# Six kinds of transposes and spreads moved from TensorE to VectorE and transfers through HBM, in a four-block transformer on one core

## The chip, the cores and the metric

The kernel runs on one core of one Trainium2 chip. The metric is the device time in microseconds, from the launch to the end of the program. The core's engines have their own instruction queues and run beside each other: TensorE (PE; its weight loads are listed as PEld), VectorE (DVE), ScalarE (ACT), GpSimd (POOL) and SyncE (SP). In this kernel SP issues all DMA transfers. An engine takes its instructions in the order written; where one waits for another engine or for a DMA, everything behind it on that engine waits too.

## The reference

The input x has 8 batches of 512 tokens of 256 float32 values. Six residual blocks follow each other:

```python
x = x + 0.5 * fp4_ffn(layernorm(x))          # gate/up/down, each operand quantised in blocks of 16
x = x + retention(layernorm(x))              # 4 blocks of 128 tokens with decay
x = x + 0.5 * fp4_ffn(layernorm(x))
x = x + 0.5 * soft_moe(layernorm(x))         # 1024 slots
x = x + attention(layernorm(x))              # 16 heads of 16, causal, low-rank additions to the weights
x = x + 0.5 * soft_moe(layernorm(x))         # the same weights again

def soft_moe(x):                             # gamma and rms norms left out
    logits   = einsum("bsd,etd->bset", xn, se)
    dispatch = softmax(logits, axis=1)                       # over the tokens
    slots    = einsum("bsd,bset->betd", xn, dispatch)
    processed = gelu(slots @ w1) @ w2
    combine  = softmax(logits.reshape(b, s, e * t), axis=-1) # over the slots
    return einsum("bnd,bsn->bsd", processed.reshape(b, e * t, d), combine)
```

## The kernel before

All matrices are float32. A batch's x stays in SBUF as 4 tiles of 128 tokens by 256 values. TensorE contracts over the partitions, so whatever was made with tokens on the partitions has to be turned before it can be contracted over its features. The kernel does this with `nc.tensor.transpose` against an identity, into PSUM, and a copy out of PSUM to SBUF.

**Three lanes.** The work of a batch is cut into units, and three lanes work on different batches at once. Lane "front" runs, for a batch, the first ffn, retention, the second ffn and the dispatch part of the first soft MoE. Lane "back" runs attention and the second dispatch. Lane "experts" runs the two large products over the slots and mixes the result back into x, for both soft MoEs. The last two batches use lanes front and back for their attention side by side. Four batches have room in SBUF; a new one is loaded when an old one has been mixed for the second time and stored.

**The order.** Instructions are written out by a planner. `Meter` keeps a modelled time of each engine; each generator step (`yield banks, needs, token`) says which PSUM rooms it wants ("p" is a pair of banks, of which there are three, "o" a single bank, of which there are two), which tokens must be done, and which token it makes. `drive` emits the next step of the lane that is able to start and has had the least of TensorE's time. Work for VectorE that may wait is kept in chains (`Chain`, `lane.later`) and put between, by `put_off`. The order is thus fixed when the program is built; on the chip each engine follows it. Every operation passes `Meter.emit`, so line 161 is the line of all instructions in the profile, and the groups are told apart by their tiles.

**The places that the change touches**, with the names of their PSUM tiles:

- `columns` (line 445): 8 transposes turn a batch's 4 tiles of 128x256 into yT, 2 x 128 x 512 (`tr_m` in dispatch, `tr_cx_a` for the context in attention; also `tr_r` in retention and `tr_a` at the head of attention), and ACT copies them out.
- `dispatch` (line 840): logits `lt` = seT by yT, with slots on the partitions. VectorE copies them to lg and takes each slot's maximum over the tokens (smax). `maxima` spreads these: `spread` transposes a column repeated 128 times, so that each partition has all slots' maxima in a row (`sm_m`). `turned` turns the logits (`l_m`), takes sm off and makes the exponentials ed. The maxima of each token over the slots (most) are spread in the same way (`nm_m`), and `less` and `combine` make the mixing weights from them. `slots(q)` makes 256 slots at a time (`sl_m`), and `slots_turned(q)` turns them with 4 transposes into slT (`slT_m`).
- `experts` (line 961): `h_e` = w1 by slT, gelu, `p_e` = w2 by that, `mo_e` mixes with lg.
- `attention` (line 1019): four rounds n of 4 heads. `largest` makes scores (`s_a`) and their maxima, negated, in a zeroed tile nmx at columns that stand for rows of q. `lower(n)` turns nmx (4 transposes, `mx_a`) and adds it to qv, so that the maximum is taken off inside the next product. `weights` makes the scores the other way round (`st_a`), then come exponentials and values (`c_a`), and `tokens_again` (`ct_a`). Finally `columns` turns the context cx, and `o_a` projects it.

Of the kernel before, what the change touches and what calls it, by code (L numbers as in the profile page):

```python
# [69 lines left out]
class Meter:  # L70
# [7 lines left out]
    BYTES, LANDS = 270e3, 1.8  # L78
    STRETCH = 3.413
    HOLE = 0.3  # L80

    def __init__(self, nc):
        self._nc = nc
        self.at = dict.fromkeys(("PE", "DVE", "ACT", "POOL", "SP"), 0.0)
        self._written, self._used = {}, {}
        self._table, self._mode = None, None
        self.end, self.last = 0.0, None
        self.moved = 0.0

        self.stretch, self.worked, self.full = self.STRETCH, 0.0, False  # L90

        self.banks = set()

        self.holds = {"DVE": [], "POOL": []}

        self.kept, self.fill = None, None
        self.tensor = _Engine(self, "PE", nc.tensor)
        self.vector = _Engine(self, "DVE", nc.vector)
        self.scalar = _Engine(self, "ACT", nc.scalar)
        self.gpsimd = _Engine(self, "POOL", nc.gpsimd)  # L100
        self.sync = _Engine(self, "SP", nc.sync)
# [10 lines left out]
    @staticmethod  # L112
    def _pieces(x):

        pitch, free = x.ap[0][0], x.ap[1:]
        first = x.offset % pitch if pitch else x.offset
        last = first + sum(s * (n - 1) for s, n in free)
        return [(x.tensor.name, k) for k in range(first // 512, last // 512 + 1)]

    def begins(self, engine, aps):  # L120

        at = self.at[engine]
        for x in aps:
            for k in self._pieces(x):
                who, t = self._written.get(k, (engine, 0.0))
                at = max(at, t if who == engine else t + self.HOP)
        for k in self._pieces(aps[0]):
            who, t = self._used.get(k, (engine, 0.0))
            at = max(at, t if who == engine else t + self.HOP)
        return at  # L130

    def emit(self, engine, op, call, args, kwargs):
# [18 lines left out]
        if engine == "SP":  # L151

            self.moved = max(self.moved, at) + int(np.prod(aps[0].shape)) * 4 / self.BYTES
            at = self.moved + self.LANDS
# [101 lines left out]
class Chain:  # L256
# [3 lines left out]
    def __init__(self, steps, needs=(), places=None):  # L260
        self.steps, self.needs, self.places = list(steps), needs, places
        self.place = None

        self.ready = 0.0

# [4 lines left out]
def macaron(ctx: ExitStack, tc: tile.TileContext, a: dict, out: bass.AP):  # L270
# [7 lines left out]
    slab = ctx.enter_context(tc.tile_pool(name="slab", bufs=1))  # L278
    ctx.enter_context(tc.manual_schedule())
# [88 lines left out]
    nmx = []  # L368
    for u in range(2):
        t = const.tile([P, NT, P], FP, tag=f"nmx{u}", name=f"nmx{u}")  # L370
        nc.gpsimd.memset(t, 0.0)
        nmx.append(t)

# [71 lines left out]
    def columns(lane, src, name):  # L445

        ps = pair(f"tr_{name}")
        for c in range(NT):
            for d in range(KD):
                nc.tensor.transpose(ps[:, d, c * P : (c + 1) * P], src[c][:, d * P : (d + 1) * P], ident)  # L450
        dst = wide(lane, f"yT_{name}", KD, S)
        nc.scalar.copy(dst, ps)
        return dst
# [37 lines left out]

    def quantise_later(lane, v, room, n, name, token, needs=()):
        def tiles(n, name):
            return [
                small.tile([P, n], FP, tag=f"{kind}{n}_{lane.name}_{chain.place}", name=f"{kind}_{name}", bufs=1)
                for kind in ("scale", "rec")
            ]

        steps = quantise_steps(v, room, n, name, tiles)
        chain = Chain([(None, step) for step in steps[:-1]] + [(token, steps[-1])], needs, lane.places)  # L500
        lane.later.append(chain)

    def project(dst, yT, w, o):

        for d in range(KD):
            nc.tensor.matmul(dst, w[:, d, o * P : (o + 1) * P], yT[:, d, :], start=(d == 0), stop=(d == KD - 1))

    def project_tokens(dst, yT, w, tiles=range(NT)):

        for t in tiles:  # L510
            for d in range(KD):
                nc.tensor.matmul(
                    dst[:, t // 2, (t % 2) * D : (t % 2 + 1) * D],
                    yT[:, d, t * P : (t + 1) * P],
                    w[:, d, :],
                    start=(d == 0),
                    stop=(d == KD - 1),
                )
# [244 lines left out]
    def retention(lane, b, after):  # L763
        nm = f"r_{b}"
        y = ys.pop(b)
        yield "p", tuple(y["tokens"]), ("yT", nm)
        yT = columns(lane, y, nm)
# [62 lines left out]
    def spread(ps, cols, n):  # L830

        for c in range(n):
            nc.tensor.transpose(ps[:, c * P : (c + 1) * P], cols[:, c : c + 1].to_broadcast([P, P]), ident)

# [5 lines left out]
    def dispatch(lane, b, tag, ep):  # L840
# [4 lines left out]
        yield "p", tuple(y["tokens"]), ("yT", nm)  # L845
        yT = columns(lane, y, nm)
# [17 lines left out]
        def maxima(h):  # L864
            ps = one(f"sm_{nm}_{h}")
            spread(ps, smax[:, h * NT : (h + 1) * NT], NT)
            sm[h] = narrow(lane, f"sm_{nm}_{h}", S)
            nc.scalar.copy(sm[h], ps)
# [20 lines left out]
        for h in range(2):  # L889
            yield "o", (("lt", nm, 2 * h), ("lt", nm, 2 * h + 1)), ("sm", nm, h)  # L890
# [6 lines left out]
        yield "o", (("ed", nm, 0, 0), ("ed", nm, 0, 1), ("ed", nm, 1, 0), ("ed", nm, 1, 1)), ("nm", nm)  # L897
        ps = one(f"nm_{nm}")
        spread(ps, most[:, 0, :], NT)
        tm = narrow(lane, f"tm_{nm}", S)  # L900
        nc.scalar.copy(tm, ps)

        def less(j):
            hs = lg[:, j : j + 2, :]
            nc.vector.tensor_tensor(hs, hs, tm.unsqueeze(1).to_broadcast([P, 2, S]), ALU.add)

        def combine(j):
# [6 lines left out]
                + [(("cw", nm) if j == NS - 2 else None, lambda j=j: combine(j)) for j in range(0, NS, 2)]  # L914
# [4 lines left out]
        def slots(q):  # L919
# [13 lines left out]
            sls[q] = narrow(lane, f"sl_{nm}_{q}", 2, D)  # L933
            for c in range(2):
                nc.vector.tensor_scalar(sls[q][:, c, :], ps[:, c, :D], rs[:, c, :], None, ALU.mult)

        def slots_turned(q):
            ps = one(f"slT_{nm}_{q}")
            for d in range(KD):
                for c in range(2):  # L940
                    nc.tensor.transpose(
                        ps[:, d * QS + c * P : d * QS + (c + 1) * P], sls[q][:, c, d * P : (d + 1) * P], ident
                    )
            slT = ep.tile([P, KD, QS], FP, tag="slT", name=f"slT_{nm}_{q}", bufs=4)
            nc.scalar.copy(slT, ps.rearrange("p (d n) -> p d n", d=KD))
            slTs.append(slT)
# [4 lines left out]
        for q in range(NQ + 1):  # L951
            if q < NQ:
                yield "p", (("nm", nm),) if q < NQ - 1 else (("cw", nm),), ("sl", nm, q)
                slots(q)
            if q:
                yield "o", (("sl", nm, q - 1),), ("slT", b, tag, q - 1)
                slots_turned(q - 1)
# [3 lines left out]
    def experts(lane, b, tag, ep):  # L961
# [4 lines left out]
        for q in range(NQ):  # L966
            hids = []
            for m in range(NH // 4):
                yield "p", (("slT", b, tag, q),), ("h", nm, q, m)
                ps = pair(f"h_{nm}_{q}_{m}")  # L970
                for c in range(4):
                    for d in range(KD):
# [3 lines left out]
                            slTs[q][:, d, :],  # L976
# [20 lines left out]
        for i in range(NT):  # L997
            yield "o", tuple(("p", nm, q) for q in range(NQ)), None
# [20 lines left out]
    def attention(lane, b, after):  # L1019
# [5 lines left out]
        yield "p", tuple(y["tokens"]), ("yT", nm)  # L1025
        yT = columns(lane, y, nm)
        qv, kv = {}, {}
# [64 lines left out]
        def largest(n, k):  # L1092

            u = n % 2
# [4 lines left out]
            ps = four(f"s_{nm}_{n}_{k}", qv[n], kv[n], parts, causalb)  # L1099
            for g in range(2):  # L1100
                for i, c in by_query[k]:
                    cols = nmx[u][:, i, :].rearrange("p (r f) -> p r f", f=32)
                    nc.vector.tensor_reduce(
                        cols[:, 2 * g : 2 * g + 2, HD * (1 - u)],
# [6 lines left out]
        def lower(n):  # L1111

            ps = one(f"mx_{nm}_{n}")
            for i in range(NT):
                nc.tensor.transpose(ps[:, i * P : (i + 1) * P], nmx[n % 2][:, i, :], ident)
            nc.vector.tensor_tensor(qv[n], qv[n], ps, ALU.add)
# [53 lines left out]
        yield "o", tuple(("s", nm, 0, k) for k in range(NK)), ("q", nm, 0)  # L1170
        lower(0)
        ctxT = None
        for n in range(N):
# [23 lines left out]
            if n + 1 < N:  # L1197
                yield "o", tuple(("s", nm, n + 1, k) for k in range(NK)), ("q", nm, n + 1)
# [3 lines left out]
        yield "p", tuple(("cx", nm, n) for n in range(N)), ("cxT", nm)  # L1202
        cxT = columns(lane, [cx[:, t, :] for t in range(NT)], f"cx_{nm}")
        for g in range(NT // 2):
            yield "o", (("cxT", nm),), None
            ps = one(f"o_{nm}_{g}")
            for t in (2 * g, 2 * g + 1):
                for d in range(KD):
                    nc.tensor.matmul(
                        ps[:, (t % 2) * D : (t % 2 + 1) * D],  # L1210
                        cxT[:, d, t * P : (t + 1) * P],
# [27 lines left out]

    def put_off(by):  # L1240
# [3 lines left out]
        for lane in lanes:  # L1244
            for chain in lane.later:
                free_place = chain.places is None or chain.place is not None or chain.places
                if chain.ready <= by and free_place and all(t in done for t in chain.needs):
                    found.append((lane, chain))
                    break
        return min(found, key=lambda x: x[0].spent, default=None)  # L1250
# [67 lines left out]
    def drive(until=lambda: False):  # L1318
        while not until():
# [6 lines left out]
            now = nc.at["PE"]  # L1326
            if nc.at["DVE"] <= now + 0.5:
# [7 lines left out]
            if ready:  # L1335
# [3 lines left out]
            found = put_off(max(nc.at["DVE"], min(first, min(  # L1339
                (c.ready for lane in lanes for c in lane.later), default=first))))  # L1340
# [99 lines left out]
```

## Time and profile before

| what | value |
|---|---|
| median of 3 runs | 3043.21 us (3041.76 to 3046.69) |
| the profiled execution's own time | 3046.74 us |
| its span, first to last instruction | 3044.9 us |
| granted TensorE clock, mean | 0.987 |
| HBM read and written | 11.87 MB, 4.19 MB |
| instructions | 36364 |

How to read it: the busy time of an engine is the union of its instructions' durations. Matmuls are pipelined, so that the mean duration of one is longer than the time by which it moves the next; a group's busy time is counted by the union. A row of the groups gives line, engine, operation, output<-inputs, shapes, count, then busy us and mean ns, then the idle time of the engine just before these instructions and what ended it. A row of the windows gives the stretch in us, its width, then the busy time of PE, PEld, DVE, ACT and POOL, each with its number of instructions, the granted clock, the DMA share and GB/s. A row of the timeline or of the chain gives start and length in us.

### The profile page before, as it was taken

The numbers are of one execution on the slowest core, as the hardware profiler recorded it, in microseconds if no ns is written. First come the engines' busy times: TensorE is split into PE (matmuls) and PEld (weight loads), VectorE is DVE, ScalarE is ACT, GpSimd is POOL, SyncE is SP. The second block draws the span as 40 slices with busy tenths as digits, with TensorE's granted clock in tenths as the row PEclk, the third lists the DMA queues.
The fourth block names the chain that finished last, engine by engine and source line by source line (L and its number), as shares of the span: only waits on it lengthen the run. The fifth ranks groups of instructions, "written<-read, shape, count | busy, mean of one in ns | idle before, by whom it ended". The sixth has DMA issues, their size and how long they took to land.

```text
span 3044.9 us, 36364 instructions
## 1 busy us (share of the span) xinstructions
PE 2913.4 (96%) x14958; PEld 2141.7 (70%) x14958; DVE 1631.3 (54%) x3767; ACT 1122.7 (37%) x1443; POOL 127.9 (4%) x231
## 2 busy tenths in 40 slices
PE   5789999999999999999999999999999999999999
PEld 3556777667776678767777678766787677675778
DVE  7676656455564563555636556465645654445240
ACT  3223433334334333433424335253443433333321
POOL 0000000000000000000000000000000000000000
PEclk8989999999999999999999999999999999999999
DMA  4000000000000000000000000000000000000000
GB/s 129 0 1 1 1 1 1 1 1 1 1 1 1 15 1 1 1 1 15 1 1 1 1 14 1 1 1 1 15 1 1 1 1 8 1 1 1 8 1 14
DMA packets 16806, 18.39 MB, mean 6 GB/s; under 512 B 2048, under 2 KB 16128, under 8 KB 16640
## 3 DMA queue, kind: packets, MB, share of 16 engines
q1 hardware_dynamic: 16640, 16.07, 1.6%
q8 instruction: 118, 1.93, 0.3%
q14 instruction: 48, 0.39, 0.0%
HBM read 11.87 MB, written 4.19 MB: 5 GB/s over the span
## 4 chain that ended last, share of the span: by engine, by line
PE 90%; DVE 6%; ACT 3%; issue 1%; SPq 0%; DMA 0%; POOL 0%; ACTq 0%; DVEq 0%; POOLq 0%
PE p_e L161 15%; PE h_e L161 14%; PE gu_f L161 10%; PE lt_m L161 7%; PE sl_m L161 7%; PE mo_e L161 7%; PE dn_f L161 5%; PE s_a L161 4%; PE st_a L161 3%; PE c_a L161 2%; PE qk_a L161 2%; PE l_m L161 1%; PE hTp_f L161 1%; PE y_r L161 1%; PE a_r L161 1%; PE k_r L161 1%
## 5 line engine op out<-in xcount | busy, mean ns | idle before, releaser
L161 PE MATMUL h_e<-slT_m,w1g 128*128 128x256 f32 x2048 | 464.9, 381 | 6.1 <-DVE nmx L161 3.1
L161 PE MATMUL p_e<-w,hid_e 128*128 128x256 f32 x2048 | 455.2, 380 | 0.9 <-DVE x L161 0.9
L161 PEld LDWEIGHTS p_e<-w,hid_e 128*128 128x128 f32 x2048 | 385.8, 190 | 64.2 <-issue 10.6
L161 PEld LDWEIGHTS h_e<-slT_m,w1g 128*128 128x128 f32 x2048 | 381.8, 190 | 67.6 <-issue 6.0
L161 PE MATMUL gu_f<-w_in,y_ffn 128*128 128x352 f32 x1024 | 334.8, 480 | 13.0 <-ACT y_ffn L161 9.7
L161 ACT ACT_TABLE_LOAD x210 | 269.4, 1283 | 109.7 <-PE h_e L161 40.0
L161 PEld LDWEIGHTS gu_f<-w_in,y_ffn 128*128 128x128 f32 x1024 | 200.1, 199 | 126.1 <-issue 17.4
L161 DVE TENSOR_REDUCE nmx<-s_a 128x2 f32<-128x256 f32 (+3 forms) x256 | 196.0, 818 | 136.8 <-PE s_a L161 136.4
L161 ACT ACTIVATE pT_a<-st_a 128x1024 f32<-128x1024 f32 (+1 forms) x192 | 158.9, 879 | 239.4 <-DVE st_a L161 222.3
L161 PE MATMUL mo_e<-proc_e,lg_m 128*128 128x257 f32 x1024 | 234.5, 382 | 1.9 <-DVE x L161 1.2
L161 ACT ACTIVATE hid_e<-h_e 128x1024 f32<-128x1024 f32 x128 | 131.0, 1023 | 277.8 <-PE h_e L161 277.6
L161 PE MATMUL sl_m<-y_dis,ed_m 128*128 128x257 f32 x1024 | 232.9, 380 | 0.1
L161 PE MATMUL lt_m<-yT_m,seT 128*128 128x512 f32 x512 | 229.7, 596 | 2.5 <-ACT yT_m L161 2.1
L161 PEld LDWEIGHTS mo_e<-proc_e,lg_m 128*128 128x128 f32 x1024 | 191.2, 190 | 35.4 <-issue 3.3
L161 PEld LDWEIGHTS sl_m<-y_dis,ed_m 128*128 128x128 f32 x1024 | 190.3, 190 | 29.8 <-issue 2.1
L161 PE MATMUL dn_f<-w_dn,hT_f 128*128 128x256 f32 x768 | 179.2, 386 | 1.2 <-DVE x L161 0.8
L161 DVE TENSOR_SCALAR_CACHE_REDUCE lg_m<-lt_m 128x512 f32<-128x512 f32 x128 | 84.5, 688 | 176.4 <-PE lt_m L161 176.3
L161 DVE TENSOR_TENSOR h_f<-h_f,gu_f 128x352 f32<-128x352 f32 x128 | 66.4, 520 | 209.9 <-ACT h_f L161 209.0
L161 PEld LDWEIGHTS lt_m<-yT_m,seT 128*128 128x128 f32 x512 | 94.8, 190 | 112.1 <-issue 100.1
L161 ACT COPY proc_e<-p_e 128x512 f32<-128x512 f32 x64 | 37.5, 586 | 351.8 <-PE p_e L161 351.8
L161 PEld LDWEIGHTS dn_f<-w_dn,hT_f 128*128 128x128 f32 x768 | 144.5, 194 | 24.0 <-DVE st_a L161 1.7
L161 DVE TENSOR_TENSOR st_a<-st_a,causalT 128x256 f32<-128x256 f32 x256 | 100.9, 428 | 96.8 <-PE st_a L161 90.3
(199 smaller groups left out, 3457.5 us busy)
## 6 DMA issues: line engine op xcount, KB each, us to landing
x<-in_L_attn_x SPq DMA_DIRECT2D x8, 512.0 KB, 5.7
out<-x SPq DMA_DIRECT2D x8, 512.0 KB, 2.9
w1g<-in_L_ffn_w SPq DMA_DIRECT2D x1, 1024.0 KB, 6.3
se<-in_L_ffn_slot_embeds SPq DMA_DIRECT2D x1, 1024.0 KB, 9.7
w<-in_L_ffn_w SPq DMA_DIRECT2D x1, 1024.0 KB, 12.2
dn<-in_L_ffn_w_down SPq DMA_DIRECT2D x1, 704.0 KB, 9.0
gu<-in_L_ffn_w_gate SPq DMA_DIRECT2D x1, 640.0 KB, 5.1
gu<-in_L_ffn_w_up SPq DMA_DIRECT2D x1, 640.0 KB, 6.4
```

The lines of the kernel that those rows point to most:

```text
L161: call(*args, **kwargs)
```

## The change

Six of the twelve kinds of transposes and spreads leave TensorE. The turning of yT in dispatch, of the context in attention and of the slots is done in blocks of 32 by 32 by VectorE (`nc.vector.transpose`), which turns each block in its place. The blocks then lie in the wrong partitions; four DMAs write them to HBM so that each row there is a row of the turned matrix, and one DMA brings it back to the same tile. The columns in the tile then have another order than before, and the products read it with steps (`tile`, `all`). The spreads of smax and most, and the maxima of attention, go out to HBM element by element as a row, and come back repeated over the partitions, or into the rows of q. In attention this replaces the addition, since the rows of q that take the maxima are written directly.

```diff
+    def through_hbm(turn, dst, n, name):
+        def away():
+            turn()
+            t["d"] = d = dram.tile([P, NB, n], FP, tag=f"d{n}", name=f"d_{name}", bufs=6)
+            z = dst().rearrange("p (b n) -> p b n", b=NB)
+            to = d.rearrange("(b i) a n -> i b a n", b=NB)
+            for k in range(NB):
+                nc.sync.dma_start(out=to[:, :, k, :], in_=z[BLK * k : BLK * (k + 1)])
+        def back():
+            nc.sync.dma_start(out=dst(), in_=t["d"].rearrange("p a n -> p (a n)"))
...
+    def spread_later(lane, cols, dst, k, needs, token, name):
+        def away():
+            t["d"] = d = dram.tile([1, P * n], FP, tag=f"row{n}", name=f"row_{name}", bufs=6)
+            nc.sync.dma_start(out=k(d), in_=cols)
+        def back():
+            nc.sync.dma_start(out=dst(), in_=t["d"].to_broadcast([P, t["d"].shape[1]]))
...
 class Columns:   # later(): what dispatch (order "d t j") and cx ("j d t") now use
+                v = self.t.rearrange(f"p (b {order}) -> p t d b j", b=NB, d=KD, t=NT)
+                for c in range(NT):
+                    blocks(v[:, c], self.src[c].rearrange("p (d b i) -> p d b i", d=KD, b=NB))
...
         def lower(n):
-            ps = one(f"mx_{nm}_{n}")
-            for i in range(NT):
-                nc.tensor.transpose(ps[:, i * P : (i + 1) * P], nmx[n % 2][:, i, :], ident)
-            nc.vector.tensor_tensor(qv[n], qv[n], ps, ALU.add)
+            def away():
+                t["d"] = d = dram.tile([NG, S], FP, tag="row_mx", name=f"row_{nm}_{n}", bufs=6)
+                nc.sync.dma_start(
+                    out=d.rearrange("r (i p) -> p (r i)", p=P), in_=nmx[n].rearrange("p r i -> p (r i)")
+                )
+            def back():
+                nc.sync.dma_start(out=qv[n][HD * (1 - n % 2) :: 32, :], in_=t["d"])
...
         def slots_turned(q):
+            def turn():
+                slT = ep.tile([P, KD * QS], FP, tag="slT", name=f"slT_{nm}_{q}", bufs=4)
+                blocks(
+                    slT.rearrange("p (n j) -> p n j", j=BLK), sls.pop(q).rearrange("p (n i) -> p n i", i=BLK)
+                )
...
-                            slTs[q][:, d, :],
+                            slTs[q].rearrange("p (a d c j) -> p d c a j", a=NB, d=KD, c=2)[:, d],
...
-                yield "p", (("nm", nm),) if q < NQ - 1 else (("cw", nm),), ("sl", nm, q)
+            yield "p", tuple(("ed", nm, q // 2, g) for g in range(2)), ("sl", nm, q)
...
-            yield "o", tuple(("p", nm, q) for q in range(NQ)), None
+            yield "o", tuple(("p", nm, q) for q in range(NQ)) + (("cw", f"m{tag}_{b}"),), None
```

The way out and the way back are two steps of a chain. Steps that only send are not treated as VectorE's work: `drive` issues them (`to_send`) as soon as, in the planner's time, their needs are there. Chains with a block transpose come before VectorE's other put-off chains (`first`). The planner's time of a transfer becomes the larger of its bytes at 270 GB/s and 3 ns for each contiguous run (`RUN`), and 1.8 us to land (`LANDS`), after the transfers before it. A row in HBM is one piece for the planner (`far`), so that the way back waits for the whole way out. The products of attention's head and of retention keep their transposes on TensorE, and so do the logits, the ffn's rows and hidden values and the context's return to tokens.

## The prediction

> **What bounds the kernel now.** I read the page first (busy shares, slices, the chain that ended last), then the groups by line, the chain of its last part, the window sums, and the DMA view and SP's timeline for what a transfer costs.
>
> ```profile
> PE 2913.4 (96%) x14958; PEld 2141.7 (70%) x14958; DVE 1631.3 (54%) x3767; ACT 1122.7 (37%) x1443; POOL 127.9 (4%) x231
> PE   5789999999999999999999999999999999999999
> PEclk8989999999999999999999999999999999999999
> PE 90%; DVE 6%; ACT 3%; issue 1%; SPq 0%; DMA 0%; POOL 0%; ACTq 0%; DVEq 0%; POOLq 0%
> ```
>
> TensorE is busy from the third slice to the last, at nearly full clock, and makes 90% of the chain. No other engine passes 54%. In the middle little is idle:
>
> ```profile
> 120.00:500.00 380.00, 350.25 (x1465) 258.63 (x1464) 241.49 (x578) 126.31 (x182) 21.07 (x37) 0.96 0.00 1
> 500.00:2500.00 2000.00, 1964.52 (x10338) 1439.67 (x10337) 1105.78 (x2558) 786.33 (x983) 83.94 (x148) 1.00 0.01 3
> 2900.00:3045.00 145.00, 139.51 (x645) 116.15 (x643) 31.80 (x71) 30.80 (x35) 1.50 (x3) 1.00 0.02 8
> ```
>
> First number after the width: PE busy. It idles 35 us in the 2000 us of the middle, 30 us between 120 and 500, 5 us at the end. A microsecond taken off TensorE is a microsecond of the end, as long as its next work is there.
>
> **What leaves TensorE.** The six kinds, by the groups (busy us and mean ns, then the idle before them):
>
> ```profile
> L161 PE MATMUL slT_m<-ident,sl_m 128*128 128x128 f32 x256 | 38.3, 275 | 3.0 <-DVE qv_a L161 0.9 <-ACT slT_m L161 0.7 <-DVE cx_a L161 0.6
> L161 PE MATMUL sm_m<-ident,smax_m 128*128 128x128 f32 x128 | 19.4, 278 | 5.3 <-DVE qv_a L161 2.3 <-ACT sm_m L161 2.0 <-DVE lg_m L161 0.5
> L161 PE MATMUL mx_a<-ident,nmx 128*128 128x128 f32 x128 | 19.4, 274 | 0.0
> L161 PE MATMUL tr_m<-ident,y_dis 128*128 128x128 f32 x128 | 16.6, 273 | 0.1
> L161 PE MATMUL nm_m<-ident,most_m 128*128 128x128 f32 x64 | 9.7, 275 | 1.0 <-DVE x L161 1.0
> L161 PE MATMUL tr_cx_a<-ident,cx_a 128*128 128x128 f32 x64 | 8.5, 274 | 0.5 <-DVE cx_a L161 0.5
> ```
>
> That is 768 transposes. What one is worth is the first choice. The mean is 274 ns, and the Trainium skill ("TensorE: Matmul & The Clock Gate", Part 4: PE-mode transpose) gives about 275 ns in a kernel: trace and page agree on the duration, which would make 768 x 0.275 = 211 us. But the durations overlap; the chain shows the time by which one moves the next:
>
> ```profile
> 2907.04 0.87 PE tr_m L161 x8
> ...
> 2911.37 13.73 PE lt_m L161 x32
> 2925.11 0.44 PE sm_m L161 x4
> ...
> 2954.86 0.44 PE slT_m L161 x4
> ```
>
> 0.87 / 8 = 0.44 / 4 = 0.109 us. So 768 x 0.109 = **83.7 us**, and that I take. The idle before these groups, 3.0 + 5.3 + 0.1 + 1.0 + 0.5 = **9.9 us**, goes with them.
>
> **What leaves and joins the others.** ACT loses the copies out of PSUM (rows: slT_m 37.0, sm_m 18.4, yT_m 16.2, tm_m 9.4, yT_cx_a 8.1: 89 us); at 37% this is worth nothing. POOL loses two memsets of 0.5 us at the start. DVE loses the 32 additions of mx_a (21.8 us) and gains block transposes: 16 x 4 and 8 x 4 of 128x256, and 64 of 128x512. No row shows one. The nearest are an SBUF-to-SBUF tensor_scalar of 128x256 (y_dis, 409 ns) and an addition of 128x512 (qv_a, 682 ns): 96 x 0.41 + 64 x 0.68 = 83 us, net +61 us, so 1692 us of about 2985, 57%. Half or double these durations makes net +20 or +144 us (60%). I take +61 and charge nothing: it runs while TensorE works for other lanes. Without that cover, each dispatch would pay 4 x 0.41 + 0.68 = 2.3 us and each attention 1.6, 50 us in all. The matmuls' count and sizes stay; only their operands' steps change (rival 3).
>
> **What SP and the DMA gain.** Each turned matrix takes four DMAs out and one back, each spread one and one: (16 + 8 + 64) x 5 + (32 + 16 + 32) x 2 = 600 issues where the program now has 48. At the 0.38 us of an x store's issue that is 228 us, on an SP that sleeps. More weighs the way back, which waits on SP until the way out has landed, with all later transfers behind it, x's loads and stores too. Durations: a 512 KB store of x lands 3.0 us after issue and a load 4.2 (the DMA view of 1000 to 1100 us); 256 KB (wT_q) 2.8; a few KB (gx) 2.1. Elements of 4 bytes are the uncertain part. The nearest row is gamma's load, which moves 4 bytes a packet (DMA view, 16.5 to 17.4 us):
>
> ```profile
> DMA packets 281, 0.00 MB, mean 1 GB/s; under 512 B 281, under 2 KB 281, under 8 KB 281
> q1 hardware_dynamic: 281, 0.00, 15.6%
> ```
>
> 0.9 us / 281 = one packet per 3.2 ns, each 0.156 x 16 x 0.9 / 281 = 8 ns of an engine: they come slower than the engines could take them. So 2048 maxima of attention take 6.6 us, 512 of dispatch 1.6. Round trips, as estimates from these rows: yT and cxT 3.5 + 4.2 = 7.7; slT, half the bytes, 6.0; a spread of dispatch 1.6 + 2.1 + 2.8 = 6.5; attention's maxima 6.6 + 2.1 + 2.1 = 10.8 us. Over 24, 64, 48 and 32 trips: 1227 us, 41% of the span even if none overlapped. SP is no bound, but a trip will sometimes queue.
>
> Those rows are loads; none shows a 4-byte store to HBM. Here a rule speaks against the change: the Trainium skill ("DMA: Bandwidth & Descriptors", Specifications) says a transfer under 512 B is a read-modify-write, and its section "Latency and other measured facts" puts an HBM access at 0.2 us. If each of the 128 writes per engine waited for that, the maxima would take 25.6 us instead of 6.6, 19 us late x 32 = 608 us. I take the row, since the engines keep many packets in flight there; below it nothing can be gained, because what paces them stays.
>
> **What covers the trips.** Maxima to weights in attention is the tightest, from the last scores (s_a) to the first weights (st_a):
>
> ```profile
> 2609.76 0.40 PE L161 MATMUL s_a<-causalb,identb 128*128 128x128 bf16 x4
> ...
> 2610.83 3.75 PE L161 MATMUL sl_m<-y_dis,ed_m 128*128 128x257 f32 x16
> 2614.41 0.60 PE L161 MATMUL mx_a<-ident,nmx 128*128 128x128 f32 x4
> ...
> 2615.28 3.64 PE L161 MATMUL sl_m<-y_dis,ed_m 128*128 128x257 f32 x16
> 2618.86 1.14 PE L161 MATMUL st_a<-qv_a,kv_a 32*128 32x512 f32 x8
> ```
>
> Already 8.8 us lie between them, filled by another lane; over all 32 such gaps the median is 8.6 us, from 3.3 to 16.9. The trip needs 10.8 us, so the order has to put one or two more groups of other lanes there. It is written out anew with the trip in it (3 ns a run, 1.8 us to land: my rows say 3.2 ns and 2.1 us), so it should. Slots no longer wait for the spread of the row maxima, only the last mixing does. yT, cxT and slT have experts' groups of 3.5 to 6.9 us beside them.
>
> I charge: 168 trips x 0.1 us = 17 us (the present hand-overs of slT_m and sm_m idle 8.3 us over 96 groups, 0.09 each); 6 us in the first dispatch, where only two lanes run; 12 us at the end, where the last dispatch has one lane of experts beside it and three of its trips (7.7 + 6.5 + 6.0 = 20 us) may outlast it. Uncovered, a trip costs its whole length.
>
> Sum: -83.7 - 9.9 + 17 + 6 + 12 = -58.6. The profiled execution took 3046.7 us (span 3044.9), so 2988; it lies 3.5 above the median of the three runs, so **2984 us**.
>
> **Rivals.** (1) *Slower: attention's maxima come late.* PE takes instructions in order; if st_a waits for q, all three lanes wait behind it. It decides when the 32 trips are late by 58.6 / 32 = 1.8 us each beyond the order's figure, i.e. if a 4-byte write takes 4.1 instead of 3.2 ns. At 5.2 ns each trip is 4 us late: 2984 + 32 x 4 = 3112 us. For it: the write has no row, and the rule above. Against: the load row has the engines at a sixth of their time.
>
> (2) *The lanes become bound by latency.* Batch 4 is loaded at 1033.2 and stored at 2517.1 us: 1484 us of life, four batches in flight, a new one only when an old one is stored. The trips add to a life about 4 x 9.7 in attention, 7.5 for cxT, 2 x 19 in the dispatches: 84 us. Were it all exposed, the period grows by 21 us, 168 us over eight batches; a quarter of it gives 2984 + 42 = 3026. For it: every lane already works through. Against: TensorE, not the lanes' waits, fills the time now, and the scheduler gives a lane that is behind the first place.
>
> (3) *The new steps in the operands cost TensorE.* h_e and lt_m now read runs of 32 floats; cxT's weights every eighth float. At 10% more, h_e (2048 x 0.216) and lt_m (512 x 0.429) lose 66 us: 3050, no gain. No row of before has such steps; runs of 128 bytes make it unlikely. At double, the 128 loads of o_a (190 ns) exceed their matmuls by 0.16: 21 us. Below nothing there is no reason.
>
> **Chances.** The forecast 0.62 (2950 to 3020), rival 1 0.18, rival 2 0.15, rival 3 0.05. A measurement of this kernel tells about 0.2%, 6 us, from no change. Faster by more: the forecast, most of rival 2: 0.75. Within: 0.04, from rivals 2 and 3. Slower: rival 1 and the bad end of 2: 0.21. Range 2945 to 3085: below, all trips are hidden and some other idle goes; above, rival 1 beyond 3 us a trip.
>
> **What would show it.** Right: PE some 84 us less busy, six groups gone, h_e and lt_m at 381 and 596 ns; about 8 us from issue to landing of the maxima's store; idle before st_a, l_m and h_e under 20 us in sum; DVE near 1690. Wrong: waits of st_a or l_m for a DMA over 50 us (rival 1), slices of PE below 9 throughout (2), longer means of h_e or lt_m (3).

## The result and the profile after

The changed kernel takes 3424.06 us (median of 4 runs, 3416.32 to 3427.10) against 3043.15 us before: 1.1246 times as long, 95% interval 1.1223 to 1.1268. I had forecast 2984 us, and 2945 to 3085 as the range. The direction was wrong, and the rival that ends on the slow side named a part of the mechanism, but less than a fifth of the loss (69 of 381 us).

The page of the kernel after, the same lines as before:

```profile
PE 2956.4 (86%) x14190; PEld 2138.8 (62%) x14190; DVE 1691.2 (49%) x3895; ACT 1099.8 (32%) x1354; POOL 127.8 (4%) x229
PE   5787999788999899878988979989799887876878
PEclk8898999899999899998999989999899999997989
PE 62%; DMA 23%; DVE 9%; ACT 3%; issue 2%; SPq 1%; POOL 0%; DVEq 0%; ACTq 0%; POOLq 0%
```

TensorE executes 768 instructions fewer and is nevertheless busy 43 us longer. The chain of which PE made 90% now has 23% of DMA in it. The sum closes on the spans, 3424.9 - 3044.9 = 380 us: TensorE's idle time rises from 131.5 to 468.5 us, +337, and its busy time by 43, which is the 83.7 us that the transposes freed and 127 us by which the rest became slower. The windows show that no stretch is spared (first after the width: PE busy; third from the end: granted clock):

```profile
500.00:3000.00 2500.00, 2211.22 (x10940) 1593.76 (x10939) 1245.94 (x2872) 834.31 (x1001) 94.09 (x162) 0.94 0.13 24
3000.00:3425.00 425.00, 334.55 (x1653) 247.12 (x1651) 124.39 (x282) 102.47 (x108) 5.97 (x12) 0.89 0.14 28
```

What TensorE waits for (total us, times, longest us; the five largest), then what SP's queue waits for, as far as it waits for a transfer to land:

```profile
PE st_a L170 <- DMA qv_a<-row_a: 124.9, 25, 7.0
PE lt_m L170 <- DMA yT_m<-d_yT_m: 54.4, 7, 13.3
PE l_m L170 <- DVE most_m L170: 46.0, 9, 9.4
PE tr_f L170 <- DVE y_ffn L170: 45.8, 15, 7.4
PE gu_f L170 <- ACT y_ffn L170: 38.6, 13, 11.0
```

```profile
SPq L170 <- DMA row_a<-nmx_a: 342.3, 32, 11.4
SPq L170 <- DMA row_sm_m<-smax_m: 293.4, 32, 11.5
SPq L170 <- DMA row_nm_m<-most_m: 99.2, 15, 10.3
SPq L170 <- DMA d_slT_m<-slT_m: 44.5, 57, 3.8
```

The second list is the key to the first. A way back cannot be issued before its way out has landed: that takes 342.3 / 32 = 10.7 us of waiting for attention's 2048 maxima, but also 293.4 / 32 = 9.2 us for the spreads of dispatch, which have only 512 elements. From issue to issue the medians in SP's timeline are 11.4 us (row_a), 9.8 (row_sm_m) and 9.8 (row_nm_m). The order counts on 8.3, 3.7 and 3.7, and my estimates were 8.7, 3.7 and 3.7. yT's blocks, with 64 times the bytes of the maxima, are hardly late: 3.9 us from the first of yT's four stores to the issue of its load (median), where my estimate for the way out was 3.5. cxT's take 10.1 all the same, because SP stands in between until a spread has landed; with the spreads back on TensorE (below) they take 3.8.

The waits for most_m and y_ffn (before: 1.4 us at l_m, 24.4 at tr_f, 9.7 at gu_f) have grown by the spreads at second hand. VectorE also takes its work in order, and it stands before ed_m and lg_m:

```profile
DVE ed_m L170 <- DMA sm_m<-row_sm_m: 135.9, 24, 12.9
DVE lg_m L170 <- DMA tm_m<-row_nm_m: 56.8, 14, 7.2
```

Behind it the other lanes' work (l_m's PSUM, the ffn's rows) waits too. The run below that has only the spreads back on TensorE shows it: there l_m waits 2.9 us for most_m, tr_f 21.8 and gu_f 5.9 for y_ffn. One stretch of the chain shows how a late trip is paid twice:

```profile
1411.88 11.26 DMA row_a<-nmx_a
...
1423.21 1.99 DMA qv_a<-row_a
...
1425.33 2.09 PE st_a L170 x8
1427.43 9.29 PE p_e L170 x32
```

The scores had ended at 1410.6. TensorE did 8 us of other work, stood idle for 6.7 us, and then the 32 matmuls of p_e took 9.29 us, where the same 32 take 6.91 us in the trace of before. p_e's operands did not change; TensorE ran slower after the gap. The clock records of the trace give 1.0 up to 1421.6 us, 0.5 from there to 1431.8, and then 1.0 again; in these two traces they have no other value. Over the program the granted clock fell from 0.987 to 0.928. TensorE was busy at 0.5 for 68.4 us before and for 320.6 us after; at half the clock, work takes twice as long, so that half of the 252 us more is lost: 126 us, which are the 127 us by which its work became slower.

### The profile page after: what moved, and what is told of

Same layout as the page of the kernel before. It is cut to its first block, busy times and chain, and to the rows that moved or that the text cites. A ratio compares the mean times of both kernels' runs of the same rounds, so it can differ in the third digit from the quotient of the medians.

```text
span 3424.9 us, 36030 instructions
## 1 busy us (share of the span) xinstructions
PE 2956.4 (86%) x14190; PEld 2138.8 (62%) x14190; DVE 1691.2 (49%) x3895; ACT 1099.8 (32%) x1354; POOL 127.8 (4%) x229
## 4 chain that ended last, share of the span: by engine, by line
PE 62%; DMA 23%; DVE 9%; ACT 3%; issue 2%; SPq 1%; POOL 0%; DVEq 0%; ACTq 0%; POOLq 0%
PE h_e L170 10%; PE p_e L170 10%; PE gu_f L170 7%; DMA row_a<-nmx_a 7%; DMA row_sm_m<-smax_m 6%; PE lt_m L170 5%; PE sl_m L170 5%; PE dn_f L170 4%; PE mo_e L170 4%; PE s_a L170 3%; PE st_a L170 3%; DMA yT_m<-d_yT_m 2%; DMA row_nm_m<-most_m 2%; DMA sm_m<-row_sm_m 2%; PE c_a L170 2%
## 5 line engine op out<-in xcount | busy, mean ns | idle before, releaser
L170 PE MATMUL h_e<-slT_m,w1g 128*128 128x256 f32 x2048 | 481.9, 392 | 33.5 <-DMA slT_m<-d_slT_m 14.1
L170 PE MATMUL p_e<-w,hid_e 128*128 128x256 f32 x2048 | 471.2, 390 | 0.9 <-DVE cx_a L170 0.3
L170 PEld LDWEIGHTS h_e<-slT_m,w1g 128*128 128x128 f32 x2048 | 397.1, 197 | 108.7 <-issue 41.1
L170 PEld LDWEIGHTS p_e<-w,hid_e 128*128 128x128 f32 x2048 | 398.8, 196 | 70.6 <-issue 13.1
L170 ACT ACT_TABLE_LOAD x257 | 329.7, 1283 | 150.9 <-PE h_e L170 68.4
L170 DVE TENSOR_REDUCE nmx_a<-s_a 128x2 f32<-128x256 f32 (+3 forms) x256 | 196.0, 818 | 205.0 <-PE s_a L170 204.4
L170 PE MATMUL lt_m<-yT_m,seT 128*128 128x512 f32 x512 | 244.5, 633 | 55.8 <-DMA yT_m<-d_yT_m 54.4
L170 PE MATMUL sl_m<-y_dis,ed_m 128*128 128x257 f32 x1024 | 247.6, 398 | 31.2 <-DVE most_m L170 29.7
L170 PEld LDWEIGHTS sl_m<-y_dis,ed_m 128*128 128x128 f32 x1024 | 202.7, 200 | 70.4 <-issue 37.6
L170 PE MATMUL st_a<-qv_a,kv_a 32*128 32x256 f32 (+3 forms) x1024 | 118.7, 540 | 127.3 <-DMA qv_a<-row_a 124.9
L170 ACT ACTIVATE ed_m<-ed_m 128x1024 f32<-128x1024 f32 x64 | 67.6, 1056 | 368.4 <-DVE ed_m L170 368.4
```

Of the source, the lines that this page charges most:

```text
L170: call(*args, **kwargs)
```

## The experiments

### A probe of the trips, and the planner's figures

The first probe copies x to the output and makes store after store, each followed by a small load that waits for it.

> A probe, no transformer: it copies x to the output and then makes store after store to HBM, each followed by a small load that waits for it, three times each. The theory ([...]those that fall in one line wait for each other): 512 stores of 4 bytes to one 2 KB row take 7 to 9 us until the load may start, 2048 to an 8 KB block 9 to 11; the same 512 with 64 or 512 bytes between them 2 to 3; 128 stores of 16 or 64 bytes 2 to 4; 16 or 64 stores of 128 bytes about 3; 512 KB in rows of 4 KB about 3. The rival, each 4-byte store costs by itself whatever lies beside it: the spaced ones take as long as the dense, 7 to 9. A 512 KB load issued beside 2048 small stores: 4 us longer than beside a 512 KB store by the first theory if they also hold up other transfers, no longer otherwise.

Its first transfers did not run in the order written: copies of x ran beside the packed and the spaced stores. With that, packed 4-byte stores took 11.0 to 11.9 us (512) and 13.6 to 13.7 (2048), 512 with 64 bytes between them 3.6 to 4.0, with 512 bytes 1.8 to 2.1. 128 rows of 16 or of 64 bytes, alone, took 1.4 us. So I repeated it in a fixed order, with more spacings.

> The probe again, with its transfers now in the order written, so that nothing runs beside a trip. 512 elements of 4 bytes packed in 2 KB; 2048 packed in 8 KB; 512 with one every 8, 16, 64 and 512 bytes; 512 pieces of 16 and of 64 bytes, packed; 512 KB in rows of 4 KB; 512 KB in four DMAs of 32 partitions; 64 runs of 128 bytes in four DMAs. Each followed by a small load that waits for it. If writes into one stretch of HBM wait for each other, the time falls as the elements move apart: 9 us packed, about half that at every second element, 2 to 3 from 64 bytes on, and pieces of 16 bytes lie in between, 3 to 5. If a write of 4 bytes costs by its size, spacing changes nothing. A 512 KB load issued after 2048 packed elements lands over 4 us later than one after rows of 4 KB.

SP's timeline of it (start us, length of the issue us). Each store is followed by the load that it had to land for, so that the difference of the starts is the trip. The first two pairs are 512 and 2048 packed elements, then 512 at every eighth and every 64th byte:

```profile
62.31 0.37 SPq L55 DMA_DIRECT2D dense<-T  x1
70.77 0.24 SPq L59 DMA_DIRECT2D T<-dense  x1
...
97.07 0.37 SPq L55 DMA_DIRECT2D dense<-T  x1
108.56 0.24 SPq L59 DMA_DIRECT2D T<-dense  x1
...
127.02 0.37 SPq L55 DMA_DIRECT2D every8b<-T  x1
130.07 0.24 SPq L59 DMA_DIRECT2D T<-every8b  x1
...
150.65 0.37 SPq L55 DMA_DIRECT2D every64b<-T  x1
152.48 0.24 SPq L59 DMA_DIRECT2D T<-every64b  x1
```

8.5 us and 11.5 us packed, 3.1 at every eighth byte, 1.8 at every 64th. 512 packed pieces of 16 bytes take 3.0 to 3.2 us, pieces of 64 bytes 1.8, and 512 KB in rows of 4 KB 2.6. (Of the four DMAs the probe tells little: the small load reads what the first of them wrote, and it starts as soon as all four are issued, after 1.7 to 2.1 us.) The size of a store alone is not what costs, since 512 spaced elements land as fast as a bulk store, and closeness alone is not, since packed pieces of 64 bytes do too; small pieces that lie close together are. And such stores hold up others. A 512 KB load issued behind 512 KB in rows, and behind 2048 packed elements:

```profile
225.75 0.42 SPq L57 DMA_DIRECT2D xx<-in_L_attn_x  x1
230.04 0.47 SPq L58 DMA_DIRECT2D T<-xx  x1
...
255.37 0.90 SPq L57 DMA_DIRECT2D xx<-in_L_attn_x  x1
269.36 0.47 SPq L58 DMA_DIRECT2D T<-xx  x1
```

4.3 us against 14.0. The 13.3 us that lt_m waited for yT, in the list above, are such a case: at 3111.7 us yT's load was issued 0.6 us after a store of row_a, and lt_m started at 3125.1.

The first experiment in the kernel tells the planner nearly the truth:

```diff
-            self.moved = max(self.moved, at) + max(bytes_ / self.BYTES, runs * self.RUN)
+            tiny = aps[0].tensor.name in self.far and bytes_ < 512 * runs
+            self.moved = max(self.moved, at) + (self.TINY + runs * self.TINY_RUN if tiny else bytes_ / self.BYTES)
```

> Only the planner's figures change: a way out in runs of under 512 bytes takes 5.3 us + 1.9 ns a run before its 1.8 us to land (8.4 us for 512 runs, 11.4 for 2048, as measured in the changed kernel), and holds the transfers behind it as long. If the loss is that the order was written for landings that come too early, it falls to 3000 to 3080 us and the granted clock returns to 0.97 or more. If the trips are simply too long to be covered, however the order is written, it stays above 3250. In between, both hold.

3307.28 us, 1.0864 (1.0846 to 1.0882). 117 of the 381 us go with the new order; 264 stay although it now counts on long trips. For the spreads it still counts on too little: 8.4 us, where their medians are 9.8 (row_sm_m) and 12.5 (row_nm_m) in this run. The waits are spread anew:

```profile
PE st_a L171 <- DMA qv_a<-row_a: 71.2, 25, 13.8
PE l_m L171 <- DVE most_m L171: 62.2, 10, 8.7
PE o_a L171 <- DMA yT_cx_a<-d_yT_cx_a: 58.4, 5, 17.1
```

Both theories hold in part. The trips are too long for the other lanes to cover, and what is behind them (cxT) is now late. How much of that comes from having all transfers on SP's queue, where a way back that waits stops every later one, no run tells: none used a second queue.

### Taking the 4-byte stores away

Maxima and spreads back on TensorE (`largest`, `lower`, `spread`, `maxima` as before), blocks kept:

> The maxima of attention and both spreads of dispatch are back on TensorE; yT, cxT and slT still go through HBM in blocks. If the 4-byte stores are the cause, 448 transposes x 0.109 = 49 us are gained and no loss is left: 2990 to 3030 us, clock 0.97 or more. If the block transfers, their five DMAs or the steps in the operands are the cause, it stays above 3200.

3082.08 us, 1.0121 (1.0106 to 1.0136). The 4-byte stores are most of the loss, but not all: 3082 is 52 us above the upper end of what I expected of their absence.

The other way to be rid of them is to keep everything off TensorE and let VectorE turn the maxima first, in a tile of 32 columns (`spread_later` and `lower` call this for the way out; the tiles of maxima get 32 columns, zeroed by GpSimd):

```diff
+    def rows_out(src, rows, d, to, name):
+        z = small.tile([P, BLK], FP, tag="z", name=f"z_{name}")
+        blocks(z, src)
+        nc.far.add(d.tensor.name)
+        for b in range(NB):
+            nc.sync.dma_start(out=to[b], in_=z[BLK * b : BLK * b + rows])
```

> The changed kernel, but the maxima are first turned in blocks of 32 by VectorE (one 128x32 transpose, 0.1 to 0.2 us), so that they leave in runs of 128 bytes, 16 or 64 of them in four DMAs, instead of 512 or 2048 of 4 bytes. If the 4-byte stores are the cause, the trips take about 6 us, as the order says, and the whole gain of the transposes comes: 2960 to 3010 us. If runs of 128 bytes are as slow[...], it stays above 3200.

3072.72 us, 1.0093 (1.0078 to 1.0108). The same 768 transposes are gone, the same trips are made and the same bytes return; the way out has runs of 128 bytes, after one transpose on VectorE of 0.2 us, and the order is written anew for that. It is 351 us faster than the changed kernel, but 63 us above the upper end of what I expected. From the first store to the way back the medians are now 2.8 us (row_a), 2.8 (row_sm_m) and 4.9 (row_nm_m), where 11.4, 9.8 and 9.8 stood. Both spreads of one dispatch, in SP's timeline, eight stores out and two ways back:

```profile
1420.80 2.72 SPq L170 DMA_DIRECT2D row_sm_m<-z_sm_m  x8
...
1424.09 0.85 SPq L170 DMA_DIRECT2D sm_m<-row_sm_m  x2
```

SP waits 25.4 us in all for row_a to land and 9.3 for row_sm_m, instead of 342.3 and 293.4. The granted clock is 0.971.

Which of the small trips cost what: only the spreads back on TensorE.

> The changed kernel with the two spreads of dispatch back on TensorE (192 transposes, 21 us); attention's maxima still leave as 4-byte elements. If each late trip costs about alike, the 48 spreads (5 us later than planned) cost more than the 32 maxima (3 us): 240 against 96 us, so about 3190. If attention's maxima are the main loss (my rival 1 as written), it stays above 3280.

3253.33 us, 1.0692 (1.0674 to 1.0710). So the spreads cost 3424 - 3253 = 171 us net of the transposes that they save and, in what is left, attention's maxima 3253 - 3082 = 171 as well. I had expected 240 and 96. TensorE waits 173.6 us for qv_a here, more than the 124.9 in the changed kernel. Next, the small stores alone, the blocks back on TensorE:

> Only maxima and spreads leave TensorE, as 4-byte elements, as in the changed kernel; yT, cxT and slT are turned on TensorE as before. 320 transposes, 35 us, leave. If the 4-byte stores cost by landing late themselves, the loss of 351 us that they make in the changed kernel (3424 against 3073 with runs) stays: about 3340. If a good part of it is that they hold up the block transfers behind them, those are gone and it takes 3150 to 3250.

3445.28 us, 1.1315 (1.1296 to 1.1333): slower than with the blocks, and 105 us above even the higher of my two figures. The 448 transposes that are back make TensorE's work about 49 us longer, and its idle time is still 440 us, against 468.5 with the blocks (55 of the 440 are new: slT's transposes, on TensorE again, wait for VectorE). So with no blocks to hold up most of the idle time stays. The hold-up, large as it is for a single load, is not what makes most of the loss; the small trips' own length is. This refutes the second reading that I had written down.

### The blocks

Only slT through HBM:

> Of the six kinds only slT goes through HBM in blocks; the other five are on TensorE as before. 256 transposes x 0.109 = 28 us leave. If the lane of experts covers these trips, as I argued, 3015 to 3025 us. If every kind that goes through HBM costs more than it frees, 3045 to 3080.

3014.02 us, 0.9900 (0.9885 to 0.9915), 1 us below what I expected: 64 trips, covered by the lane of experts, and the kernel gains about 30 us (1 - 0.9900 of 3046 us on that chip), the 28 of its transposes and a little more. With maxima and spreads in runs added, and yT and cxT left on TensorE:

> slT in blocks, and maxima and spreads in runs of 128 bytes; yT in dispatch and cxT are back on TensorE. 576 transposes x 0.109 = 63 us leave. If the remaining 30 us over before of the kernel with runs come from yT and cxT (idle 17 + 12 us before lt_m and o_a, and o_a's slower loads), it takes 2990 to 3020 us and beats the kernel before. If they come from the trips in general (the lanes' waits and the lower clock after each gap), 3040 to 3070.

2993.20 us, 0.9827 (0.9813 to 0.9842), at the lower end of what I expected. This version beats both kernels. Its page:

```profile
PE 2849.6 (95%) x14382; PEld 2081.6 (70%) x14382; DVE 1665.4 (56%) x3879; ACT 1123.6 (38%) x1377; POOL 134.0 (4%) x309
```

2913.4 - 576 x 0.109 = 2850.6: TensorE's busy time is what the sum of the prediction makes it, at a granted clock of 0.989. Idle is 144 us, 12 above before. So 53 of the 63 us arrive at the end (3045.9 us before, on that chip). What remained were yT and cxT, alone:

> The kernel with runs, with yT of dispatch back on TensorE and cxT still through HBM: 640 transposes, 70 us, leave. Against the best kernel so far (2993) it differs in cxT alone. If a trip costs where no other lane has work, as the trace of the kernel with runs shows before o_a at 1427 us, it loses some 10 to 30 us in one or two such places and o_a's loads, strided, cost 5: 3000 to 3030. If trips are covered, 2986 to 2993.

> The kernel with runs, with cxT back on TensorE and yT of dispatch still through HBM: 704 transposes, 77 us, leave. Against 2993 it differs in yT alone, 16 trips at a point where the lane can do nothing else. By the same theory it loses 40 to 60 us: 3030 to 3055. If yT's trips are covered, 2979 to 2993, and then the two together must be what hurts.

cxT in blocks: 3009.21 us, 0.9887 (0.9872 to 0.9902). yT in blocks: 3022.32 us, 0.9927 (0.9912 to 0.9941). The first lies where I expected it; the second lies between my two figures and so fits neither. They cost about 16 and 29 us (18 and 30 by the ratios), but together 80 (3073 against 2993). The stretch where the two kernels differ most, first with both in blocks, then with neither:

```profile
1000.00:1500.00 500.00, 448.89 (x2150) 319.97 (x2149) 268.19 (x651) 165.90 (x197) 20.07 (x48) 0.95 0.13 35
...
1000.00:1500.00 500.00, 495.16 (x2491) 371.38 (x2490) 299.66 (x699) 201.04 (x239) 22.78 (x51) 1.00 0.10 27
```

TensorE's timeline in it, with both in blocks (in brackets the idle time before, and what ended it):

```profile
1412.72 3.60 PE L170 MATMUL lt_m<-yT_m,seT 128*128 128x512 f32 x8
1427.39 3.77 PE L170 MATMUL o_a<-effo,yT_cx_a 128*128 128x256 f32 x8 [11.07 <-DMA yT_cx_a<-d_yT_cx_a]
...
1437.97 14.15 PE L170 MATMUL sl_m<-y_dis,ed_m 128*128 128x257 f32 x64 [0.87 <-DVE most_m L170]
1460.72 9.76 PE L170 MATMUL h_e<-slT_m,w1g 128*128 128x256 f32 x32 [8.59 <-DMA slT_m<-d_slT_m]
```

There, attention waits for cxT (sent at 1419.0), the dispatch of another batch for its spread (sent at 1420.8), and the experts have no slots yet: no lane has work for TensorE, and later again, when slT is under way. I took this for a lack of batches, since the front lane loads a new one only when an old one is stored, and gave it a fifth:

> The kernel with runs (all six kinds moved, 3073 us), with room for five batches of x instead of four, so that the front lane may load and start the next batch one mixing earlier; some small buffers are fewer to make the room. If yT's and cxT's trips cost because at times no lane has anything to do while they are under way, the front lane's extra work covers them and it falls to 2980 to 3020 us. If a trip costs wherever it stands, it stays at 3055 to 3085.

> The best kernel so far (slT in blocks, maxima and spreads in runs, yT and cxT on TensorE, 2993 us) with the same fifth batch. It has little idle left to cover (144 us, most of it at the start): 2980 to 2996 us by the first theory as by the second.

With the fifth batch and all six kinds moved: 3046.75 us, 1.0011 (1.0004 to 1.0018), 26 us less than with four. Without yT and cxT: 2992.77 us, 0.9838 (0.9823 to 0.9852), no change. Neither of the two figures for the first was met, and the stretch from 1000 to 1500 us is as idle as before, 448.7 us busy of 500. SP's timelines show that room was not what was lacking in it. With four places the fifth batch's load was issued at 1070.1 us, 63 us after the store that made room for it (1007.2); with five places it needs no store and was still issued only at 1064.6. In the kernel before, the load follows the store by 3 us. So the fifth place helps a little, elsewhere, and does not test the theory where it mattered. That the two kinds cost more together than alone is shown; why the order lets their trips coincide is not.

## Why the prediction was wrong, point by point

**What a transposition is worth: right.** 0.109 us, not 0.275. Where the trips were covered, the busy time fell by about that: by 30.6 us with slT alone, where the sum says 27.9, and by 63.8 in the best version, where it says 62.8.

**VectorE and ScalarE: right, in part by luck.** The block transposes kept VectorE busy for 45.0 us for slT (706 ns each), 22.7 for yT (411) and 16.2 for cxT (621): 84 us against my 83, and DVE is busy 1691 us against my 1692. The row of slT:

```profile
L170 DVE STREAM_TRANSPOSE slT_m<-sl_m 128x512 f32<-128x512 f32 x64 | 45.0, 706 | 1.5
```

The sum is closer than the estimate deserved: cxT's, whose output is strided, take 621 ns and not 409, but durations of neighbours overlap (yT's 64 x 411 ns would be 26.3 us).

**The 4-byte stores: the step that failed.** I wrote "I take the row", and put gamma's load of 4-byte elements in the place of a store to HBM. A load of 4-byte elements writes them into different partitions of SBUF; the stores here pack them into rows of 2 KB in HBM. Between the ends that I had named for attention's maxima, 8.7 and 27.7 us with the landing, it was neither: 11.5 us in the probe and 11.4 in the kernel. And I applied the doubt to attention alone. The 512 elements of a spread, which I priced at 3.7 us, take 8.5 alone and 9.8 in the kernel. So 48 trips more than I had counted were late, and by more: 6 us each against 3. The argument for the row, that what paces the packets stays, fails too: of a store of 2048 elements all packets had run 2.3 us after its issue, and the landing came 9 us later (last section). The Trainium skill ("DMA: Bandwidth & Descriptors", Specifications), with its read-modify-write under 512 bytes, pointed the right way, and I set it aside; but its boundary is not what the runs show either. Packed pieces of 64 bytes, and single elements 64 bytes apart, land in 1.8 to 2.0 us.

**"168 trips x 0.1 us": the size that failed with it.** I put 17 us for all trips. The waits for DMAs at st_a and lt_m alone are 179 us, and what VectorE passes on to other lanes comes on top; the idle time grew by 337 us in all. I had asked who waits for st_a, and not who waits for VectorE while it waits for sm and tm.

**The price of a gap: left out.** Rival 1 priced a late trip at its lateness: 32 x 4 us, 3112. After a gap of 6.7 us the next 7 us of matmuls took 2.4 us longer. Over the program that is the 126 us at half the clock beside 337 us of added idle, more than a third on top. TensorE was busy at half the clock for 139.5 us in the kernel with runs and for 62.0 in the best one, whose idle time is near that of before.

**Covered by other lanes: right for slT and the runs, half right for yT and cxT.** Trips that land in time are covered nearly everywhere (2993 us), but two kinds more make 80 us, most of it in the middle of the program, through coincidences that the 8.6 us of the median gap could not show. My charge of 6 + 12 us for the first and last dispatch was right: with yT in blocks TensorE waits 6.3 us for it in the first dispatch (at 263 us), and in the last 5.9 for yT (2903 us) and 7.5 behind the spread (2929 us). What I had at nothing was the middle.

**Rival 2** does not stand by itself. Batch 4 lives 1632 us in the changed kernel, against 1484 before, which is 10% more in a program that is 12% longer. In the kernel with runs, with as many trips, it lives 1455 us.

**Rival 3** is small. My sign for it, longer means of h_e and lt_m, came up in the changed kernel (392 and 633 ns), but with the clock: at 0.97 or more h_e takes 381 to 387 ns with the steps, against 381 before, and lt_m 606 to 612 with them and 596 to 606 without. o_a's weight loads rose from 190 to 335 ns, and the group from 29.3 to 32.5 us busy with cxT alone in blocks: 3 us, against the 21 us that I gave for double.

## What to carry to other kernels

Price a transfer by a row that has its target, its direction and its packing, and where there is none, measure it alone before building on it: 512 elements packed in HBM took 8.5 us, three times as long as 512 KB in rows (2.6). If a few values per partition have to become a row, turn them on VectorE first, so that they leave in runs: it changed 3424 us into 3073. When TensorE is the bound, add to every exposed wait the slower matmuls after it (here 126 us beside 337), and ask for every wait on any in-order engine which other lanes stand behind it.

## What the runs showed of the hardware that I had not expected

Packed 4-byte stores to HBM take 8.5 us for 512 and 11.5 us for 2048. The packets themselves are short: of one store of row_a, issued at 593.38 us, whose way back was issued at 605.10, the view of the DMA's activity in 40 slices of 0.29 us shows

```profile
DMA  0003777600000000000000300000000000000000
DMA packets 2065, 0.02 MB, mean 2 GB/s; under 512 B 2064, under 2 KB 2064, under 8 KB 2064
```

All of its packets have run by the eighth slice, 2.3 us after the issue; in the 9.4 us after that no packet of it is seen (the 3 in the middle is one packet of another queue), and the queue waits for it all the same. What the memory does in that time no view shows. Every second word alone takes 3.1 us, and packed stores of 16 bytes 3.0. While packed elements are under way, a load of 512 KB from elsewhere lands 9.7 us later; its packets are spread over the whole 14 us (the probe from 255 to 270 us), so that it crawls rather than stands. 512 elements scattered within SBUF land in 2.0 to 2.1 us.
